# Attention's residual kept in its token tile, scaled and shifted on GpSimd, without the identity products behind Wo

## The chip, the cores and the metric

The kernel runs on one core of a Trainium2 chip (trn2). The metric is the device time of one execution in microseconds, as the median of several runs; shorter is better. Beside it stands the profile of one execution on that core, with every instruction of the five engines in time: TensorE (PE, with its weight loads as PEld), VectorE (DVE), ScalarE (ACT), GpSimd (POOL), and SyncE (SP), which issues most of the DMA.

## What is computed

Sixteen samples, each 256 tokens of 256 values in fp32, go through four layers one after the other. Only the second one changes here:

```
L0:  x = layernorm(x + up(expert(gelu(down(x))))) * gamma + beta     # an expert per sample
L1:  emb = silu(sin_emb(timestep)) @ W_ada + b_ada                   # (16, 512)
     scale, shift = split(emb)                                       # per sample, per value
     x = layernorm(x) * (1 + scale) + shift
     scores = (x Wq + bq)(x Wk + bk)^T / 4 + attention_bias ; masked ; softmax   # 16 heads
     x = x + (softmax(scores) (x Wv + bv)) @ Wo + bo                 # the residual in question
     x = x + gelu2(layernorm2(x) @ W1 + b1) @ W2 + b2
L2:  x = layernorm(x + one of three MLPs, chosen per sample) * gamma + beta
L3:  x = relu(x + dt * (derivatives of A*x and B*x on the 256x256 grid))
```

The attention bias is a side input of 16 x 16 x 256 x 256 fp32 values, 64 MB, read once.

## The kernel before

Weights stay on chip; a sample is two chunks of 128 tokens, so a tile [128, 2, 256] holds it ("token tile": tokens on partitions), and its transpose holds values on partitions. The work is written as generators, one per stage, which run over the 16 samples: `prepare` (L0 and the normalization of L1), `project` (q, k, v), `weigh` (scores, bias, softmax, over 64 groups of four heads), `attend` (transposing the weights and multiplying by v), `divide` (the softmax's division, the product with Wo and the residual; one call for each half of the heads), `enter` and `feed` (the MLP of L1), `end` (L2) and `step` (L3).

The order of instructions on all engines is fixed while the program is built. A planner, the class `Flow` (L91 to L167), keeps an estimated clock for each engine and for 7 of the PSUM banks; a generator yields the time from which it can go on, or a condition on `done`, and `flow.add(stage, at, per)` (L1103 to L1110) gives each stage an offset and a rate that decide which goes first. The estimates that stages report (`flow.pe(2.6)` and such) only make the order. On the chip each engine runs its list in that order and waits for semaphores. DMA issues are part of the same lists: SP issues the loads of x, expert weights, bias tiles (`load_side`), masks and branch weights and the stores of the output, ACT the first weights, and POOL the transfers that add the mask to a bias tile in place (`add_mask`, L508).

Lines that the change touches:
- `condition` (L486) computes scale and shift for all samples with values on partitions (`ps_a`, L491), `conditioned` (L500) adds the bias into `ada`.
- `prepare` normalizes x into `c_ln` (L567, 2 copies; it waits until `project` has transposed the tile of two samples before).
- `project` transposes it (`c_t`) and ACT applies scale and shift on the way out of PSUM (`c_xt`, L583, 3 copies). From `c_xt` come q, k and v. A gate (L577) holds it until the residual of three samples before is finished.
- `divide` uses `c_xt` a second time. The residual is needed with tokens on partitions, so it is transposed back by adding to the product with Wo:

```
for k in range(NC):                                                   # L814
    nc.tensor.matmul(ps_o[:, c, :], c_t[:, k, tok_], wo[:, k, :], start=k == 0, stop=False)
for k in range(NC):                                                   # L816
    nc.tensor.matmul(ps_o[:, c, k * P : (k + 1) * P], x_t[:, k, tok_], ident, start=False, ...)
```

- DVE then adds `bo` (L828) into `y`, a token tile of 4 copies, and takes its statistics; POOL computes the root and bias of the norm (L411 to L415). A gate (L810) holds `divide` until `step` of four samples before is done.

At the start, idle products (`idle`, L215) keep TensorE running while the first data come.

Of the kernel before, what the change touches and what calls it, by code (L numbers as in the profile page):

```python
# [19 lines left out]
P = 128  # L20
# [150 lines left out]
def chain_kernel(ctx: ExitStack, tc: tile.TileContext, t: dict, out: bass.AP):  # L171
# [31 lines left out]
        return at  # L203

    SIDES = 3
    xp = ctx.enter_context(tc.tile_pool(name="xp", bufs=2))
    side = ctx.enter_context(tc.tile_pool(name="side", bufs=SIDES))

# [42 lines left out]

    w_ada = wp.tile([P, NC, 2 * D], F32, name="w_ada", tag="d_w", bufs=1)
    nc.scalar.dma_start(out=w_ada, in_=chunked(t["W_ada"]))
    smalls = hp.tile([P, NC * S], F32, name="smalls", tag="d_ln", bufs=1)
    used = [0]

# [224 lines left out]
        nc.vector.tensor_copy(e_add, ps_b)  # L481
        return free("ps_b", flow.dve(0.2, flow.pe(0.5)))

    ps_a = {}

    def condition():  # L486

        ps_a[0] = misc("ps_a", [P, 4, B])
        for m in range(4):
            for k in range(NC):  # L490
                nc.tensor.matmul(  # L491
                    ps_a[0][:, m, :],
                    w_ada[:, k, m * P : (m + 1) * P],
                    silu[:, k, :],
                    start=k == 0,
                    stop=k == NC - 1,
                )
        flow.pe(2.0)

    def conditioned():  # L500
        nc.vector.tensor_tensor(ada, ps_a.pop(0), b_ada.unsqueeze(2).to_broadcast([P, 4, B]), ALU.add)
# [14 lines left out]
    def prepare():  # L516
        for b in range(B):
            w = e_ws.pop(b)
            xx = xs.pop(b)
            x, xt = xx[:, :, :D], xx[:, :, D:]  # L520
            ps_h = misc(f"a_h{b}", [A, S])
            for k in range(NC):
                nc.tensor.matmul(ps_h, w_down[:, k, :], xt[:, k, :], start=k == 0, stop=k == NC - 1)
            h1 = xp.tile([A, S], F32, name=f"a_h1{b}", tag="a_h1", bufs=1)
            nc.scalar.activation(h1, ps_h, AF.Gelu, bias=columns("down_b")[:A])
# [24 lines left out]
            nc.vector.tensor_tensor(x, ps_u, x, ALU.add)  # L550
            at = free(f"a_u{b}", flow.dve(0.7, flow.pe(0.9)))
            stat, at = take_stats(f"0_{b}", x, at)
            if b == 0:
                condition()
                idle(512, 512)
            yield at, 0
            tmp = xp.tile([P, NC, D], F32, name=f"b_tmp{b}", tag="b_tmp", bufs=1)
            at = normalized_affine(x, x, stat, ln0_g, ln0_b, tmp, b == 0)
            yield at, 0
            stat, at = take_stats(f"1_{b}", x, at)  # L560
            if b == 0:
                conditioned()
                masked.update((m, 0.0) for m in range(4))
            yield at, 0
            if b > 1:
                yield lambda: ("turned", b - 2) in done
            ln = xp.tile([P, NC, D], F32, name=f"c_ln{b}", tag="c_ln", bufs=2)  # L567
            lns[b] = ln, normalized(ln, x, stat, b == 0)
            done.add(("normal", b))

    def project():
        for b in range(B):
            yield lambda: ("normal", b) in done
            ln, at = lns.pop(b)
            yield at
            if b > 2:
                yield lambda: ("finish", b - 3) in done  # L577
            ps_t = misc(f"c_t{b}", [P, NC, S])
            at = transposed(ps_t, ln)
            done.add(("turned", b))  # L580
            x_t = wp.tile([P, NC, S], F32, name=f"c_xt{b}", tag="c_xt", bufs=3)
            for k in range(NC):
                nc.scalar.activation(  # L583
                    x_t[:, k, :],
# [47 lines left out]
            ready[b] = x_t, qz, k_t, va, sums  # L632
            done.add(("prepare", b))
            yield 0.0
            if b > 1:
# [29 lines left out]
    PR = 6  # L665
    MASK_FROM, MASK_BY = 2, 1

    def weigh():

        at = 0.0  # L670
        for m, (b, half, par) in enumerate(QUADS):
            if m % 4 == 0:
                yield lambda: ("prepare", b) in done
            _, qz, k_t, _, sums = ready[b]
            ps = []
            for i in range(4):
                yield 0.0, 1
# [70 lines left out]
    def attend():  # L748
        for m, (b, half, par) in enumerate(QUADS):
            if m % 4 == 0:  # L750
                yield lambda: ("values", b) in done
            for i in range(4):
                n = 4 * m + i
                yield lambda: ("weigh", n) in done
                pr, at = weights.pop(n)
                yield at
                ps_p = misc(f"c_pt{n}", [P, NC, S])
                at = transposed(ps_p, pr)
                p_t = hp.tile([P, NC, S], F32, name=f"c_pts{n}", tag="c_pts", bufs=4)
# [9 lines left out]
            ps_c, va = ctxs[b, half], ready[b][3]  # L769
            for k in range(NC):  # L770
                for i in range(4):
                    nc.tensor.matmul(  # L772
                        ps_c[32 * i : 32 * i + 32, :],
                        va[:, k, 4 * half + i, 2 * par : 2 * par + 2, :].rearrange("p e d -> p (e d)"),
                        turned[i][:, k, :],
                        start=par == 0 and k == 0,
                        stop=par == 1 and k == NC - 1,
                    )
            at = flow.pe(1.06)
            done.add(("gather", m))  # L780
            if par == 1:
                flow.add(divide(b, half), -9.0, 1e9)
            yield 0.0, 0

    def divide(b, half):


        x_t, _, _, _, sums = ready[b]
# [16 lines left out]
        done.add(("divide", 2 * b + half))  # L805
        yield flow.dve(0.34, at)
        if half == 0:
            return
        if b > 3:
            yield lambda: ("step", b - 4) in done  # L810
        ps_o = misc(f"c_o{b}", [P, NC, D])
        for c in range(NC):
            tok_ = slice(c * P, (c + 1) * P)
            for k in range(NC):  # L814
                nc.tensor.matmul(ps_o[:, c, :], c_t[:, k, tok_], wo[:, k, :], start=k == 0, stop=False)
            for k in range(NC):  # L816
                nc.tensor.matmul(
                    ps_o[:, c, k * P : (k + 1) * P],
                    x_t[:, k, tok_],
                    ident,  # L820
                    start=False,
                    stop=k == NC - 1,
                )
        at = flow.pe(2.6)
        del ready[b], c_ts[b]
        y = xp.tile([P, NC, D], F32, name=f"y{b}", tag="y", bufs=4)
        for c in range(NC):
            nc.vector.tensor_tensor(y[:, c, :], ps_o[:, c, :], bo, ALU.add)  # L828
        at = free(f"c_o{b}", flow.dve(0.67, at))
        stat, at = take_stats(f"2_{b}", y, at)  # L830
        ys[b], stats2[b] = y, (stat, at)
        done.add(("finish", b))
# [267 lines left out]
                    )  # L1100
                yield 0.0

    flow.add(prepare(), -2.56, 2.25)  # L1103
    flow.add(project(), -0.82, 5.7)
    flow.add(weigh(), 0, 21.2)
    flow.add(attend(), 0.96, 11.3)
    flow.add(enter(), -0.26, 0.44)
    flow.add(feed(), 2.45, 13.9)
    flow.add(end(), 2.77, 3.95)
    flow.add(step(), 4.22, 7.0)  # L1110
    flow.run()

def _arrays(inputs):
# [17 lines left out]
    for n in ("b_ada", "bq", "bk", "b1", "g2", "beta2"):  # L1131
# [21 lines left out]
        ),  # L1153
        "rows_a": np.concatenate([l0["ln_gamma"], l0["ln_beta"], l1["bv"], l1["bo"]]),
        "rows_b": np.concatenate([l1["b2"], l2["gamma"], l2["beta"], v["condB_dt"]]),
        **{k: l1[k] for k in ("W_ada", "Wo", "W1", "W2")},
        "W_qkv": np.concatenate([l1["Wq"], l1["Wk"], l1["Wv"]], 1),
        "W_branch": np.stack(
# [33 lines left out]
```

## Time and profile before

| | us |
|---|---|
| median of 3 runs (lowest, highest) | 923.14 (921.53, 926.4) |
| the profiled execution | 919.35 |
| its span, first to last instruction | 917.5 |
| mean granted TensorE clock in it | 0.990 of full speed |

The same lines group as follows in the profile (busy time is a union over time; the mean is that of one record, and an fp32 product leaves two records):

| group | records | busy us | mean ns |
|---|---|---|---|
| L815 PE, product with Wo | 128 | 33.8 | 387 |
| L817 PE, identity products | 128 | 19.5 | 275 |
| L828 DVE, y = c_o + bo, 128x256 | 32 | 12.1 | 419 |
| L583 ACT, c_xt from c_t, 128x256 | 32 | 16.0 | 550 |
| L446, L447 POOL on x, 128x512 | 15, 15 | 24.0, 19.1 | 1603, 1274 |
| L508 POOL, mask transfers issued | 60 | 80.8 | 1355 |

A line of busy times names the engine, its busy time and share, and the number of instructions. In a line of waits come the engine and line that stood still, what ended the wait, and the total, the number and the longest of these waits in us. A line of the list in order of time has the start, the time taken, engine, line, operation and tiles, and in brackets the idle time before it with what ended it. A line by stretch has the stretch, its length, the busy time of each engine with its number of instructions in parentheses, and at its end the granted clock, the share of DMA and GB/s.

### The profile page before, as it was taken

How to read it: one execution, taken by the hardware profiler on the slowest of the kernel's cores; microseconds unless marked ns; L12 is line 12 of the kernel's file. 1: busy time of each engine (PE TensorE's matmuls, PEld its weight loads, DVE VectorE, ACT ScalarE, POOL GpSimd, SP SyncE). 2: the span in 40 equal slices, each digit the busy share in tenths (PEclk: the TensorE clock that was granted, in tenths of full speed). 3: DMA queues.
4: the chain of work that ended last, by engine and by line, in shares of the span. 5: the costliest groups of instructions: out<-in, count | busy, mean ns of one | idle time of the engine just before them, and what ended most of it. 6: DMA issues, size and time to landing. Idle time of an engine off the chain costs nothing. (4 is left out here: it accounts for less than half of the span.)

```text
span 917.5 us, 18282 instructions
## 1 busy us (share of the span) xinstructions
PE 885.9 (97%) x6180; PEld 698.2 (76%) x6180; DVE 639.5 (70%) x2110; ACT 568.6 (62%) x1561; POOL 357.1 (39%) x500
## 2 busy tenths in 40 slices
PE   8899998999999999999999999999999999999997
PEld 3567675887777887778788777877887788778885
DVE  6677767767785767677686777768777785766343
ACT  2576667667665766758576675847667576656330
POOL 2233329142632616245261614526161543422331
PEclk8999999999999999999999999999999999999999
DMA  9389887776596767949676794967678486861010
GB/s 292 102 241 326 231 217 193 203 206 184 139 239 171 185 184 183 228 127 242 170 176 179 189 247 114 238 171 170 178 204 208 124 206 173 213 149 42 1 41 24
DMA packets 126555, 163.05 MB, mean 178 GB/s; under 512 B 12455, under 2 KB 86266, under 8 KB 126458
## 3 DMA queue, kind: packets, MB, share of 16 engines
q0 software_dynamic: 31680, 62.92, 34.1%
q1 hardware_dynamic: 93568, 96.92, 32.5%
q10 hardware_dynamic: 1209, 1.99, 0.7%
q8 instruction: 52, 0.85, 0.4%
q14 instruction: 46, 0.37, 0.1%
HBM read 94.69 MB, written 4.19 MB: 108 GB/s over the span
## 5 line engine op out<-in xcount | busy, mean ns | idle before, releaser
L718 ACT ACTIVATE c_pr<-c_sc,c_mx 128x256 f32<-128x256 f32 x512 | 255.1, 500 | 179.6 <-DVE c_mx L707 178.7
L707 DVE CUSTOM_DVE_ANT_0 c_sc<-c_s,side 128x256 f32<-128x256 f32 x512 | 194.4, 417 | 28.3 <-ACT e_o L1096 7.7
L454 PE MATMUL c_pt<-ident,c_pr 128*128 128x128 f32 x1024 | 143.5, 278 | 7.0 <-ACT c_pr L718 5.2
L454 PEld LDWEIGHTS c_pt<-ident,c_pr 128*128 128x128 f32 x1024 | 116.6, 142 | 34.6 <-ACT c_pr L718 12.7
L462 DVE COPY c_pts<-c_pt 128x512 f32<-128x512 f32 x183 | 122.8, 685 | 27.7 <-PE c_pt L454 27.4
L508 POOL DMA_DIRECT2D side<-neg x60 | 80.8, 1355 | 143.9 <-DMA side<-in_side 70.4
L411 POOL TENSOR_SCALAR rs<-mv 128x2 f32<-128x2 f32 x64 | 14.2, 221 | 293.6 <-DVE mv L408 291.7
L873 PE MATMUL d_f<-d_ht,w 128*128 128x256 f32 x512 | 121.4, 381 | 0.1
L903 PE MATMUL d_o<-w,d_z 128*128 128x256 f32 x512 | 116.0, 380 | 0.0
L903 PEld LDWEIGHTS d_o<-w,d_z 128*128 128x128 f32 x512 | 95.0, 190 | 12.3 <-issue 0.4
L873 PEld LDWEIGHTS d_f<-d_ht,w 128*128 128x128 f32 x512 | 92.8, 190 | 11.9 <-issue 0.9
L718 ACT ACTIVATION_READ_ACCUMULATOR c_pr<-c_sc,c_mx 128x1 f32 x512 | 96.1, 188 | 0.0
L689 PE MATMUL c_s<-c_kt,c_qz 32*128 32x256 f32 x1024 | 76.6, 401 | 0.8 <-DVE c_mx L707 0.4
L772 PE MATMUL c_c<-c_pts,c_va 128*32 128x256 f32 x1024 | 72.0, 387 | 3.3 <-DVE c_pts L462 2.9
L689 PEld LDWEIGHTS c_s<-c_kt,c_qz 32*128 32x128 f32 x1024 | 47.9, 184 | 23.5 <-issue 15.8
L892 ACT ACTIVATE d_f<-d_z 128x512 f32<-128x512 f32 x64 | 38.2, 597 | 28.5 <-DVE d_z L889 27.7
L772 PEld LDWEIGHTS c_c<-c_pts,c_va 128*32 128x32 f32 x1024 | 27.5, 109 | 33.4 <-issue 16.1
L911 DVE SCALAR_TENSOR_TENSOR y<-d_o,y 128x256 f32<-128x256 f32 x32 | 13.6, 424 | 55.5 <-PE d_o L903 55.5
L889 DVE TENSOR_SCALAR d_z<-d_f,cols 128x256 f32<-128x256 f32 x102 | 44.5, 477 | 10.7 <-PE d_f L873 9.9
L412 POOL TENSOR_TENSOR rs<-rs,inv_sqrt 128x2 f32<-128x2 f32 x64 | 46.0, 719 | 5.3
L464 ACT COPY c_pts<-c_pt 128x512 f32<-128x512 f32 x73 | 41.7, 572 | 8.8 <-PE c_pt L454 7.7
L896 DVE SCALAR_TENSOR_TENSOR d_z<-d_f,d_z 128x512 f32<-128x512 f32 x64 | 43.1, 673 | 3.5 <-ACT d_f L892 3.5
(152 smaller groups left out, 1602.2 us busy)
## 6 DMA issues: line engine op xcount, KB each, us to landing
side<-in_side SPq DMA_DIRECT2D x256, 256.0 KB, 5.6
side<-neg POOLq DMA_DIRECT2D x60, 1024.0 KB, 8.4
x<-in_x SPq DMA_DIRECT2D x16, 512.0 KB, 5.6
d_w<-in_W_branch SPq DMA_DIRECT2D x16, 512.0 KB, 6.4
out<-e_o SPq DMA_DIRECT2D x15, 256.0 KB, 4.9
w<-in_W SPq DMA_DIRECT2D x2, 1024.0 KB, 7.5
d_bout<-in_bl_branch SPq DMA_DIRECT2D x16, 128.0 KB, 5.8
grids<-in_grids SPq DMA_DIRECT2D x1, 1792.0 KB
```

What stands on the lines that cost most here:

```text
L412: nc.gpsimd.tensor_tensor(rs, rs, inv_sqrt, ALU.pow)
L454: nc.tensor.transpose(ps[:, k, c * P : (c + 1) * P], src[:, c, k * P : (k + 1) * P], ident)
L462: nc.vector.tensor_copy(dst, ps)
L508: nc.gpsimd.dma_start(out=sides[m].rearrange("p (h c) k -> p h (c k)", h=HB), in_=negs[m // 4].rearrange("p c k -> p (c k)").unsqueeze(1). ...
L689: nc.tensor.matmul(ps[i][:, c, :], qz[rows32, par, half, c * P : (c + 1) * P], k_t[rows32, half, :], start=b > 0, stop=b > 0 or c == NC - 1,)
L707: nc.vector.tensor_tensor_reduce(out=sc[:, c, :], in0=ps[i][:, c, :], in1=sb[:, i * NC + c, :], scale=-1.0, scalar=3.0e38, op0=ALU.add, op ...
L718: nc.scalar.activation(pr[:, c, :], sc[:, c, :], AF.Exp, bias=mx[:, c : c + 1], scale=-1.0, accum_out=sums[:, c, h : h + 1],)
L772: nc.tensor.matmul(ps_c[32 * i : 32 * i + 32, :], va[:, k, 4 * half + i, 2 * par : 2 * par + 2, :].rearrange("p e d -> p (e d)"), turned[i ...
L873: nc.tensor.matmul(ps_f[:, i, :], w1[:, k, f * P : (f + 1) * P], h_t[:, k, :], start=k == 0, stop=k == NC - 1,)
L889: nc.vector.tensor_scalar(z[:, i, :], ps_f[:, i, :], b1[:, f : f + 1], None, ALU.add)
L896: nc.vector.scalar_tensor_tensor(z, ps_f, 1.0, z, ALU.add, ALU.mult)
L903: nc.tensor.matmul(ps_o, us[f // 2][:, f % 2, c * P : (c + 1) * P], w2[:, f, :], start=f == 0, stop=f == NF - 1,)
```

## The change

The normalized token tile itself becomes the residual. It is no longer a tile of its own (`c_ln`) but the later `y`, with 7 copies. POOL multiplies it by (1 + scale) and adds shift + bo, both as rows that are the same on all partitions, when the first half of the heads is divided. For that, scale and shift are computed a second time, with samples on partitions: two products of 512 columns (`ps_r`) in `condition`; `modulated` adds 1, `b_ada` and `bo` on DVE, stores the 16 rows of 512 values to a DRAM scratch tensor and loads row 0 back, broadcast to 128 partitions; both DMAs are issued by ACT. The rows of later samples are loaded by SP in `divide`, one sample ahead, into one buffer. The product with Wo is alone in its accumulation, and DVE adds `ps_o` and `y` in one operation of 512 columns. Three gates between stages fall, one is added for the 7 copies, `c_xt` goes from 3 to 2 copies, and the offsets of six stages are set anew; so the planner's order changes throughout.

```diff
+    PR = 6
+    TOKENS = 7
+    dp = ctx.enter_context(tc.tile_pool(name="dp", bufs=1, space=bass.MemoryType.DRAM))
+    row_store = dp.tile([B, 2 * D], F32, name="row_store", tag="row_store")
...
     nc.scalar.dma_start(out=w_ada, in_=chunked(t["W_ada"]))
+    mod_rows = hp.tile([P, 2 * D], F32, name="mod_rows", tag="c_pr", bufs=PR)[:B]
+    nc.scalar.dma_start(out=mod_rows, in_=t["b_ada_row"].partition_broadcast(B))
...
-        flow.pe(2.0)
+        ps_r[0] = misc("ps_r", [P, 2 * D])
+        for k in range(NC):
+            nc.tensor.matmul(ps_r[0][:B], silu[:, k, :], w_ada[:, k, :], start=k == 0, stop=k == NC - 1)
+        flow.pe(3.8)
+
+    def modulated():
+
+        row, got = mod_rows, ps_r.pop(0)[:B]
+        nc.vector.scalar_tensor_tensor(row[:, :D], got[:, :D], 1.0, row[:, :D], ALU.add, ALU.add)
+        nc.vector.tensor_tensor(row[:, D:], got[:, D:], row[:, D:], ALU.add)
+        free("ps_r", flow.dve(0.8))
+        nc.vector.tensor_tensor(row[:, D:], row[:, D:], bo[:B], ALU.add)
+        flow.dve(0.4)
+        nc.scalar.dma_start(out=row_store, in_=row)
+        load_row(0, nc.scalar)
+
+    def load_row(b, engine):
+        mods[b] = wp.tile([P, 2 * D], F32, name=f"row{b}", tag="row", bufs=1)
+        engine.dma_start(out=mods[b], in_=row_store[b : b + 1, :].rearrange("b n -> (b n)").partition_broadcast(P))
...
-            if b > 1:
-                yield lambda: ("turned", b - 2) in done
-            ln = xp.tile([P, NC, D], F32, name=f"c_ln{b}", tag="c_ln", bufs=2)
+            if b >= TOKENS:
+                yield lambda: ("step", b - TOKENS) in done
+
+            ln = xp.tile([P, NC, D], F32, name=f"y{b}", tag="y", bufs=TOKENS)
             lns[b] = ln, normalized(ln, x, stat, b == 0)
+            if b == 0:
+                modulated()
...
-            if b > 2:
-                yield lambda: ("finish", b - 3) in done
...
-            x_t = wp.tile([P, NC, S], F32, name=f"c_xt{b}", tag="c_xt", bufs=3)
+            tokens[b] = ln
+            x_t = wp.tile([P, NC, S], F32, name=f"c_xt{b}", tag="c_xt", bufs=2)
...
         if half == 0:
+
+            y, row = tokens[b], mods.pop(b)
+            both = [P, NC, D]
+            nc.gpsimd.tensor_tensor(y, y, row[:, :D].unsqueeze(1).to_broadcast(both), ALU.mult)
+            nc.gpsimd.tensor_tensor(y, y, row[:, D:].unsqueeze(1).to_broadcast(both), ALU.add)
+            flow.pool(2.7)
             return
-        if b > 3:
-            yield lambda: ("step", b - 4) in done
+        if b + 1 < B:
+            load_row(b + 1, nc.sync)
...
             for k in range(NC):
-                nc.tensor.matmul(ps_o[:, c, :], c_t[:, k, tok_], wo[:, k, :], start=k == 0, stop=False)
-            for k in range(NC):
                 nc.tensor.matmul(
-                    ps_o[:, c, k * P : (k + 1) * P],
-                    x_t[:, k, tok_],
-                    ident,
-                    start=False,
-                    stop=k == NC - 1,
-                )
-        at = flow.pe(2.6)
+                    ps_o[:, c, :], c_t[:, k, tok_], wo[:, k, :], start=k == 0, stop=k == NC - 1
+                )
+        at = flow.pe(1.75)
...
-        y = xp.tile([P, NC, D], F32, name=f"y{b}", tag="y", bufs=4)
-        for c in range(NC):
-            nc.vector.tensor_tensor(y[:, c, :], ps_o[:, c, :], bo, ALU.add)
-        at = free(f"c_o{b}", flow.dve(0.67, at))
+        y = tokens.pop(b)
+        nc.vector.tensor_tensor(y, ps_o, y, ALU.add)
+        at = free(f"c_o{b}", flow.dve(0.68, at))
...
-    flow.add(prepare(), -2.56, 2.25)
-    flow.add(project(), -0.82, 5.7)
+    flow.add(prepare(), -2.54, 2.25)
+    flow.add(project(), -0.62, 5.7)
...
-    flow.add(attend(), 0.96, 11.3)
-    flow.add(enter(), -0.26, 0.44)
-    flow.add(feed(), 2.45, 13.9)
-    flow.add(end(), 2.77, 3.95)
-    flow.add(step(), 4.22, 7.0)
+    flow.add(attend(), 0.71, 11.3)
+    flow.add(enter(), -0.23, 0.44)
+    flow.add(feed(), 3.38, 13.9)
+    flow.add(end(), 2.6, 3.95)
+    flow.add(step(), 5.13, 7.0)
```

More of the change, by code (lines that the diff above doesn't have):

```diff
@@ L482, in expert_bias @@
         return free("ps_b", flow.dve(0.2, flow.pe(0.5)))
-    ps_a = {}
+    ps_a, ps_r, tokens, mods = {}, {}, {}, {}
     def condition():
@@ L575, in project @@
             yield at
-            if b > 2:
-                yield lambda: ("finish", b - 3) in done
             ps_t = misc(f"c_t{b}", [P, NC, S])
             at = transposed(ps_t, ln)
-            done.add(("turned", b))
-            x_t = wp.tile([P, NC, S], F32, name=f"c_xt{b}", tag="c_xt", bufs=3)
+            tokens[b] = ln
+            x_t = wp.tile([P, NC, S], F32, name=f"c_xt{b}", tag="c_xt", bufs=2)
             for k in range(NC):
@@ L631, in project @@
             sums = wp.tile([P, NC, H], F32, name=f"c_sum{b}", tag="c_sum")
-            ready[b] = x_t, qz, k_t, va, sums
+            ready[b] = qz, k_t, va, sums
             done.add(("prepare", b))
@@ L664, in chain_kernel @@
     weights, turned, c_ts, ctxs = {}, {}, {}, {}
-    PR = 6
     MASK_FROM, MASK_BY = 2, 1
@@ L673, in weigh @@
                 yield lambda: ("prepare", b) in done
-            _, qz, k_t, _, sums = ready[b]
+            qz, k_t, _, sums = ready[b]
             ps = []
@@ L768, in attend @@
                 ctxs[b, half] = pp.tile([P, S], F32, name=f"c_c{b}_{half}", tag="c_c", bufs=1)
-            ps_c, va = ctxs[b, half], ready[b][3]
+            ps_c, va = ctxs[b, half], ready[b][2]
             for k in range(NC):
@@ L785, in divide @@
     def divide(b, half):
-        x_t, _, _, _, sums = ready[b]
+        _, _, _, sums = ready[b]
         ps_c = ctxs.pop((b, half))
@@ L1155, in _arrays @@
         "rows_b": np.concatenate([l1["b2"], l2["gamma"], l2["beta"], v["condB_dt"]]),
+        "b_ada_row": l1["b_ada"],
         **{k: l1[k] for k in ("W_ada", "Wo", "W1", "W2")},
```

## The prediction

> **What bounds the kernel now.** I read the busy table first, then busy time by stage, then who waited for whom, and last the list of instructions in order of time around the lines that change. Engine, busy time with its share of the span, instructions:
>
> ```profile
> PE 885.9 (97%) x6180; PEld 698.2 (76%) x6180; DVE 639.5 (70%) x2110; ACT 568.6 (62%) x1561; POOL 357.1 (39%) x500
> ```
>
> TensorE (PE) is busy for 885.9 of 917.5 us, which leaves 31.6 us without a matmul. By stage (stretch, its length, then busy time of PE, PEld, DVE, ACT and POOL):
>
> ```profile
> 0.00:24.00 24.00, 19.94 (x56) 9.36 (x56) 15.98 (x65) 7.18 (x11) 5.99 (x19) 0.86 0.91 289
> 24.00:40.00 16.00, 13.70 (x80) 9.96 (x84) 9.37 (x31) 7.86 (x23) 2.94 (x6) 0.89 0.06 18
> 100.00:200.00 100.00, 94.43 (x679) 71.73 (x678) 71.47 (x249) 68.12 (x193) 42.76 (x57) 0.98 0.76 197
> 500.00:600.00 100.00, 99.32 (x731) 80.07 (x729) 73.98 (x248) 68.25 (x185) 45.31 (x62) 1.00 0.75 188
> ```
>
> From 300 us on TensorE rests for under 1 us in 100. The holes are in the start, in the filling of the pipeline up to about 300, and at the end. Busy matmul time could hide a stall, because matmuls are pipelined, so I ask what PE waited for:
>
> ```profile
> PE c_pt L454 <- ACT c_pr L718: 5.2, 11, 1.8
> PE e_t L454 <- POOL y L447: 2.9, 2, 2.2
> PE c_c L772 <- DVE c_pts L462: 2.9, 4, 1.1
> ```
>
> All waits named for PE add up to some 26 us, and the largest is 5.2. ACT, DVE and POOL wait for each other far longer (ACT 178.7 us for the row minima of L707), but with slack. So the body is bound by the amount of matmul work in order, and a microsecond taken from it there should shorten the span. The start is different: a chain across ACT, DVE and PE sets it.
>
> **What the Trainium skill says.** "Perfetto Trace Analysis", section Identifying the Most-Contended Engine, warns that matmul occupancy is no measure of roofline and prefers the share of weight loads. Here that is 76%, and the list of waits, not the 97%, is what my reading rests on. "TensorE: Matmul & The Clock Gate", section Architectural detail, says that ACT and DVE are strict first-in first-out; the trace agrees, since ACT's first table load comes only after the held-back issue of w_qkv (7.04 to 7.44). "DMA: Bandwidth & Descriptors", section Anatomy of one DMA, puts about 2 us of fixed cost on a DMA, most of it the receipt of the write, and says that the issuing sequencer does the waiting; the fastest write in this trace (128 KB of out) lands in 1.7 us. "GPSIMD Engine Reference", section Key points, says that GpSimd shares its SBUF interfaces with DVE; L446 on 128x512 took 1270 ns at least and 1762 in the median, L447 1273, which fits.
>
> **The change, part by part.**
>
> Removed from PE: 8 identity products per sample. Their busy time, 19.5 us, counts overlap. The true pitch is read from PE in order of time:
>
> ```profile
> 857.10 1.03 PE L815 MATMUL c_o<-wo,c_cts 128*128 128x256 f32 x4
> 857.96 0.61 PE L817 MATMUL c_o<-ident,c_xt 128*128 128x128 f32 x4
> 858.41 1.03 PE L815 MATMUL c_o<-wo,c_cts 128*128 128x256 f32 x4
> 859.27 0.61 PE L817 MATMUL c_o<-ident,c_xt 128*128 128x128 f32 x4
> 859.72 3.62 PE L903 MATMUL d_o<-w,d_z 128*128 128x256 f32 x16
> ```
>
> From 857.96 to 858.41 is 0.45, and from 859.27 to 859.72 again. Two per sample, 16 samples: 2 x 0.45 x 16 = 14.4 us off PE.
>
> Added to PE at the start: ps_r, two products of 512 columns. The idle products of that width on L222 took 0.94 a pass at a slow clock (3.76 us for 4 passes), and 8 passes of 256 columns at full clock take 1.89, or 0.47 for 512. So 1.9 to 3.8 us. I take the upper, and hide it behind DVE's norm chain, which ends at 21.27 while ps_r would end near 20.3. If DVE were quicker, it would show on c_t, which PE could still start between 22 and 27.5 (see next).
>
> Added to ACT at the start, in front of everything else. Of the lines for ACT:
>
> ```profile
> 13.38 1.28 ACT L525 ACT_TABLE_LOAD   x1
> 21.77 0.47 ACT L525 ACTIVATE a_h<-a_h,cols 64x256 f32<-64x256 f32 x1 [7.10 <-PE a_h L523]
> 23.44 1.02 ACT L583 ACTIVATE c_xt<-c_t,ada 128x256 f32<-128x256 f32 x2 [1.21 <-PE c_t L454]
> ```
>
> In the new order the store of the 16 rows and the load of row 0 stand on ACT's queue between the tanh of the time embedding and this table load. The store waits for DVE's last row operation. The load waits until the store has landed in DRAM. Behind them wait the Gelu table, a_h of sample 1 and c_xt of sample 0, and behind c_xt all projections. Step by step:
> - The b_ada load takes an earlier slot in ACT's DMA order, and the builder makes rows_a and w_qkv wait for older transfers (x of sample 0 and w_ada). w_ada, issued at 2.74, lands 5.5 later, about 8.3; the first Gelu table then starts near 9.1 instead of 7.53 and the Gelu about 0.5 later than 9.72: +0.5 (0 to 1).
> - Three DVE operations on 16x256 behind c_ln, priced by the 128x256 row of L828 (419 ns): 1.3. Rows are ready at 21.27 + 0.5 + 1.3 = 23.1.
> - Store: 2.5 from issue to landing (1.7 is the fastest write seen, 4.9 the median of out): 25.6. Issue of the load 0.4: 26.0.
> - Table load 1.28, Gelu 0.47: c_xt at 27.7, against 23.44. That is **+4.3 us**, from 3 to 7.
>
> Moved at the start: the score products of sample 0 now stand before c_v, which before came first (PE 27.64 to 29.5). Scores wait only for c_kt, which ACT finishes at 28.88 while they began at 30.33. And c_v (1.89) now lies where PE stood idle 2.3 us between 24 and 40. I take -1.5 (0 to -2.3).
>
> DVE: 32 additions of 0.419 become 16 of about 0.69 (as y at L1028): -2.4 us. The written order also turns 31 copies c_pts from ACT to DVE (+21.2) and 22 d_z from DVE to ACT (-10.5); with the smaller ones DVE gains about 11 us, ACT loses about 7. DVE then has 650 of some 906, 72%: not on the path, because PE waited for it about 7 us after the start.
>
> POOL: 2 operations of 128x512 per sample, each 1.27 to 1.79, so 2.5 to 3.6 a pair, 41 to 57 us in all; POOL goes from 39% to about 45%. Nothing: they stand half a sample (some 27 us of PE work between the two divisions) ahead of the addition that reads them. Behind a pair on POOL's queue stand most often the root and the bias of the third norm, then a mask transfer, and for those the cover is PE work too: by PE's order, at the durations above, d_y to e_t has 40 to 56 us in the body (50.9 before).
>
> DMA: 16 row loads of 256 KB (4.2 of 163 MB), 15 on SP. Each takes an issue slot (0.4) ahead of a side load, and waits for POOL's pair of the sample before. SP stood 392.9 us waiting for DVE at L307, so the slot is free; the row has half a sample to land, rows_a took 5.0. If the row came late, POOL would stop and every norm with it.
>
> Buffers and waits: the token tile has 7 copies, three gates fall, c_xt goes to 2. I read the cover between producers and consumers off both PE orders: d_t to d_f rises from 7.6 to about 19 us, c_t to c_q from 2.4 to about 4.9, c_r to c_o from 1.0 to 3.5; d_g to d_y falls from 4.1 to about 3, a_h to a_e is shorter early, and two places (c_r to c_o of samples 0 and 14) have only 0.6. I take 0 for new and lost stalls, from -4 to +8. The end is the same sequence from d_f of sample 15 on: 0.
>
> Sum: -14.4 + 4.3 - 1.5 + 0 = **-11.6 us**. Span 917.5 becomes 905.9; the execution 919.35, with 1.85 around its span, becomes 907.8. The median of the three runs, 923.14, is 3.8 above the profiled one; I carry the difference over: **911.5 us**.
>
> **The rivals.**
> 1. Start and body both dearer: store and load 4.9 each way in effect (+7), stalls +3 to +5. -14.4 + 7 - 0.5 + 3 = -5, up to -1: 918 to 922. For it: landing under load in this trace is mostly 4 to 6. Against: the queues are near empty from 24 us on (DMA share 0.06).
> 2. Slower: POOL's pair stands in front of a norm that PE needs. At the root of a norm (L411) POOL so far arrives early, and waits 291.7 us for DVE. If of each pair's 2.9 us some 1.5 comes through to PE per sample, 24 us are lost and the sum is +12: 935. It decides from 11.6 / 16 = 0.73 us per sample on (no gain), and is slower by 0.5% from 1.0. Against: e_t waited for POOL only about 5.6 us in all, and the cover above.
> 3. The gain does not arrive: ACT and DVE set the pace, PE merely idles more. It gives 923 + 2.8 = 926. Against: PE waited for them for a few us.
> 4. More gain: the fuller cover takes away part of the 10 us of stalls between 60 and 300: down to 904 or less.
>
> **How the numbers follow.** Main case 0.58 (906 to 917), rival 1 0.16, rival 2 0.12, rival 3 0.05, rival 4 0.09. About 0.5% (4.6 us) is what a measurement can tell from no change. Faster, below 918.5: main, rival 4, and a fifth of rival 1: 0.70. Same: the rest of rival 1 and half of rival 3: 0.16. Slower: 0.14. Range: 904 leaves out half of rival 4, 926 leaves out rival 2 and half of 3: 904 to 926.
>
> **What would show it.** Right: PE has no 128x128 identity rows on c_o, and its busy sum is about 16 to 18 us less; c_xt starts near 27.7 with ACT waiting for the store; PE stays above 99% from 300 to 700; the addition of y is not held by POOL. Wrong: PE waits for POOL's norms or for y above 10 us in all; POOL waits for the row load; PE between 100 and 700 falls below 98%; or c_xt starts after 31.

## The result, and the profile after

The changed kernel takes 929.65 us in the median of six runs (926.77 to 932.13), the kernel before 923.29 beside it. The ratio is 1.0065, with a 95% interval of 1.0044 to 1.0086: slower by about 6.4 us, where 11.6 us less were forecast. The profiled execution took 926.77 us with a span of 925.0 (before 919.35 and 917.5).

The busy table of the kernel after (engine, busy time with its share of the span, instructions):

```profile
PE 886.4 (96%) x6056; PEld 680.6 (74%) x6056; DVE 657.7 (71%) x2106; ACT 563.6 (61%) x1552; POOL 399.1 (43%) x532
```

TensorE (PE) has 124 instructions fewer, and its busy time has not fallen at all (885.9 before). The removed products did go: measured from one PE start to the next, they cost 14.5 us in the trace of before, and there is nothing in their place after. In order of time at the end of the run, the product of Wo now goes straight on into d_o:

```profile
866.36 1.89 PE L845 MATMUL c_o<-wo,c_cts 128*128 128x256 f32 x8
868.08 4.26 PE L926 MATMUL d_o<-w,d_z 128*128 128x256 f32 x19
```

So more time passes at other groups of products. The same sums from start to start, which hold the wait before the next product too, name them: c_q +6.8, c_t +4.4, c_s +3.7, ps_r +3.5 (new), d_o +2.7, c_k +2.4, c_pt and c_o +1.9 each. By stage (the same stretches and columns as before the change: busy time of PE, PEld, DVE, ACT, POOL; granted PE clock; DMA share; GB/s):

```profile
0.00:24.00 24.00, 19.48 (x53) 9.13 (x54) 16.15 (x65) 4.87 (x7) 6.00 (x19) 0.86 0.89 281
24.00:40.00 16.00, 12.65 (x58) 9.06 (x59) 3.08 (x12) 6.91 (x13) 0.00 (x0) 0.79 0.15 49
...
100.00:200.00 100.00, 96.37 (x670) 73.17 (x671) 79.49 (x261) 68.67 (x197) 47.18 (x62) 0.98 0.82 214
...
500.00:600.00 100.00, 98.71 (x706) 76.25 (x705) 72.21 (x233) 65.57 (x185) 49.98 (x64) 1.00 0.76 195
```

Two things are to be seen. From 24 to 40 us PE starts 58 matmuls where it started 80, and its clock is lower (0.79; 0.89 before). And from 500 to 600 it rests for 1.29 us instead of 0.68. What PE waited for, of the whole run:

```profile
PE c_pt L460 <- ACT c_pr L742: 3.7, 10, 1.5
PE a_e L564 <- ACT a_h L549: 3.6, 2, 3.3
PE c_k L622 <- DVE c_mx L731: 3.0, 1, 3.0
```

The second is new, 3.3 us in one piece at the start, and so is the third, 3.0 us in one piece at 98 us, to which section 4 of the experiments comes back.

**The start.** ScalarE (ACT) in order of time:

```profile
22.55 0.33 ACTq L517 DMA_DIRECT2D row_store<-mod_rows  x1
26.57 0.35 ACTq L522 DMA_DIRECT2D row<-row_store  x1
26.95 1.28 ACT L549 ACT_TABLE_LOAD   x1 [13.46 <-DMA row_store<-mod_rows]
28.25 0.47 ACT L549 ACTIVATE a_h<-a_h,cols 64x256 f32<-64x256 f32 x1
28.62 1.01 ACT L608 ACTIVATE c_xt<-c_t,ada 128x256 f32<-128x256 f32 x2
```

The chain is the one of the prediction, link by link. The rows were ready earlier than forecast (22.55 for 23.1), the store took 4.0 us until the load could be issued (2.5 forecast), and c_xt began at 28.62 (27.7 forecast, 23.44 before). TensorE behind it:

```profile
28.77 1.11 PE L564 MATMUL a_e<-a_h,e_w 64*64 64x256 f32 x2 [3.35 <-ACT a_h L549]
29.82 3.78 PE L622 MATMUL c_q<-c_xt,w_qkv 128*128 128x256 f32 x8
33.39 2.63 PE L622 MATMUL c_k<-c_xt,w_qkv 128*128 128x256 f32 x8
```

Before, the eight products c_q took 2.02 and c_k 1.89. After the rest of 3.35 us they step at 427 ns, and from the fifth of c_k on at 216: the clock was halved for some 12 products, which is 2.5 us more. "TensorE: Matmul & The Clock Gate" of the Trainium skill (Part 1: The HAM clock gate) says that an idle window of about 3.4 us brings the half clock; this rest agrees with the size, others in these traces do not (last section). The first score products c_s start at 36.83, 6.5 us later than before (30.33), though c_v no longer stands ahead of them.

**The body.** Between 300 and 700 us, what the weight loads (PEld) of c_pt, the transposes of the softmax, sat idle for. In the kernel before:

```profile
L454 PEld LDWEIGHTS c_pt<-ident,c_pr x472: 138/141/144, 300.0 to 696.1; 128*128 128x128 f32 x158
its engine sat idle before it (us, times) until:
  issue: 2.9, 7
```

In the kernel after:

```profile
L460 PEld LDWEIGHTS c_pt<-ident,c_pr x478: 137/140/143, 300.5 to 699.9; 128*128 128x128 f32 x160
its engine sat idle before it (us, times) until:
  issue: 9.7, 26
  DVE c_mx L731: 4.6, 10
  ACT c_pr L742: 3.5, 9
  ACT d_z L910: 2.1, 6
  ACT c_spr L817: 1.9, 5
  ACT c_pts L470: 1.0, 3
```

Most of this is no loss. When c_c, c_s or a_h comes ahead of c_pt, the weight load rests 0.41, 0.33 or 0.38 us, whatever the profile names, and with the same lengths in half_both below: the 2.9 us before are seven times 0.41 behind c_c, and after nearly all but the line of c_mx has these three lengths. The new order puts c_pt behind such products more often, and other products less; c_c and c_s themselves take 16.0 and 17.2 us in four steady samples in both orders, from start to start. The waits for c_mx are another matter. With two more, in order of time:

```profile
397.42 0.86 PEld L460 LDWEIGHTS c_pt<-ident,c_pr 128*128 128x128 f32 x8 [0.45 <-DVE c_mx L731]
398.73 0.42 PEld L460 LDWEIGHTS d_t<-ident,d_ln 128*128 128x128 f32 x4 [0.46 <-DVE d_z L919]
399.50 1.59 PEld L665 LDWEIGHTS c_v<-w_qkv,c_xt 128*128 128x128 f32 x8 [0.34 <-ACT c_kt L653]
422.41 0.42 PEld L460 LDWEIGHTS c_pt<-ident,c_pr 128*128 128x128 f32 x4 [0.47 <-DVE c_mx L731]
```

These four waits come once in each of five samples and set their product back by 0.21, 0.39, 0.27 and 0.40 us, 1.27 us a sample. None waits for its input: the softmax that c_pt reads had been ready for 8.3 and 4.0 us, d_ln for 0.65, and c_v reads c_xt, which c_q and c_k had read before. What they wait for is the accumulator, the PSUM bank that they write into. By the planner's allotment of its seven PSUM banks, these c_pt get the bank of a score product c_s, d_t that of a d_f, c_v that of c_k, and c_mx, d_z and c_kt, which the profile names, are what reads those banks out. Between 300 and 700 us no product of the kernel before waits in this way.

None of this stands high in a list of waits. Its effect is read from the period, the time between the starts of c_q of neighbouring samples. Of four samples, c_q (min, median and max of one product in ns, then the first and the last start) before:

```profile
L597 PE MATMUL c_q<-c_xt,w_qkv x32: 379/379/380, 431.6 to 593.0; 128*128 128x256 f32 x32
```

and after:

```profile
L622 PE MATMUL c_q<-c_xt,w_qkv x32: 379/379/483, 447.8 to 611.2; 128*128 128x256 f32 x32
```

From the first start to the last (three periods and the 1.5 us within a sample) it was 161.4 us and is 163.4. A sample takes 53.25 us before and 54.1 after (four periods from 339 to 556 us; the third here is already 53.6), though it has 0.9 us of products less: 1.75 us per steady sample are lost, and the four waits above are 1.27 of them.

### The profile page after: what moved, and what is told of

It reads as the page before. It is cut to its first block, busy times and chain, and to the rows that moved or that the text cites. A ratio compares the mean times of both kernels' runs of the same rounds, so it can differ in the third digit from the quotient of the medians.

```text
span 925.0 us, 18078 instructions
## 1 busy us (share of the span) xinstructions
PE 886.4 (96%) x6056; PEld 680.6 (74%) x6056; DVE 657.7 (71%) x2106; ACT 563.6 (61%) x1552; POOL 399.1 (43%) x532
## 5 line engine op out<-in xcount | busy, mean ns | idle before, releaser
L460 PE MATMUL c_pt<-ident,c_pr 128*128 128x128 f32 x1024 | 150.6, 280 | 5.6 <-ACT c_pr L742 3.7
L460 PEld LDWEIGHTS c_pt<-ident,c_pr 128*128 128x128 f32 x1024 | 112.9, 141 | 55.0 <-issue 21.5
L468 DVE COPY c_pts<-c_pt 128x512 f32<-128x512 f32 x214 | 143.8, 685 | 12.2 <-PE c_pt L460 11.0
L713 PE MATMUL c_s<-c_kt,c_qz 32*128 32x256 f32 x1024 | 78.6, 408 | 4.2 <-DVE c_mx L731 1.8
L713 PEld LDWEIGHTS c_s<-c_kt,c_qz 32*128 32x128 f32 x1024 | 49.6, 187 | 27.2 <-issue 11.3
L731 DVE DVE_READ_ACCUMULATOR2_ANT c_mx<- 128x1 f32 x512 | 42.8, 84 | 0.0
L1001 POOL TENSOR_TENSOR y<-y,d_bout 128x256 f32<-128x256 f32 x32 | 26.7, 981 | 30.8 <-PE d_t L460 20.9
```

The lines of the kernel that those rows point to most:

```text
L460: nc.tensor.transpose(ps[:, k, c * P : (c + 1) * P], src[:, c, k * P : (k + 1) * P], ident)
L468: nc.vector.tensor_copy(dst, ps)
L713: nc.tensor.matmul(ps[i][:, c, :], qz[rows32, par, half, c * P : (c + 1) * P], k_t[rows32, half, :], start=b > 0, stop=b > 0 or c == NC - 1,)
L731: nc.vector.tensor_tensor_reduce(out=sc[:, c, :], in0=ps[i][:, c, :], in1=sb[:, i * NC + c, :], scale=-1.0, scalar=3.0e38, op0=ALU.add, op ...
```

## The experiments

Three theories went in. A: the new written order of TensorE's work loses the gain. B: GpSimd's pair of operations comes in front of norms that PE needs. C: the start, held by the store and the load on ScalarE's queue. All ratios are to the kernel before.

**1. Which of the three.** `new_old_order` is the whole change with the planner's estimates, gates and start offsets of before, and PE's order is then that of before, less the identity products:

```
+ flow.pe(2.6) at Wo, flow.pe(2.0) at ps_r; no flow.pool for the pair, none for the rows
+ gates ("turned", b-2), ("finish", b-3), ("step", b-4) as before
+ flow.add offsets -2.56, -0.82, 0, 0.96, -0.26, 2.45, 2.77, 4.22
```

> The changed residual (token tile, GpSimd pair, rows from DRAM, no identity products) with the planner's estimates, gates and offsets of the kernel before, so that TensorE's order is that of the kernel before without the identity products. Theory A (the new order of instructions loses the gain, some 1.7 us per sample): the gain comes back, less the longer start: 923.3 - 14.4 + 6.5 = about 915 us, 912 to 919. Theory B (the GpSimd pair itself costs, by holding up norms and masks or VectorE's port): no better than the changed kernel, 926 to 931. Theory C (the start alone is what is wrong): about 917 as well, so A and C are told apart by the period of a sample: under A 52.4 us here against 54.1 in the changed kernel, under C the same in both.

Measured: 917.79 us, ratio 0.9940 (0.9923 to 0.9957). It is faster than before, and 11.9 us faster than the change as made, by what the planner writes alone: the order, and with it the engine of some copies. `ident_new_order` turns it round, the order of after with the work of before:

```
- nc.gpsimd.tensor_tensor(y, y, row...) x2
+ identity products with c_xt (3 copies) behind Wo; bo added by VectorE in two operations
+ row loads of half the size, not read
```

> The changed kernel's order, with the identity products put back behind Wo, bo added by VectorE in two operations, and the GpSimd pair left out (the row loads stay, at half the size, and nobody reads them). Theory A: the order is what is slow, and TensorE in it has slack of its own: identity products cost 14.4 us at most, and less where TensorE waits for the softmax: 936 to 944 us. Theory B: products back (+14.4) and the pair's cost gone (some 15): about 929.

Measured: 937.65, 1.0145 (1.0112 to 1.0179), with a period of 54.9 us against 53.25. The start with the store and load is in this time too; the period is not touched by it. A holds in both directions. `no_pair` is the change without GpSimd's two operations (the scale and shift of the residual are left out):

```
- nc.gpsimd.tensor_tensor(y, y, row[:, :D]..., ALU.mult)
- nc.gpsimd.tensor_tensor(y, y, row[:, D:]..., ALU.add)
```

> The changed kernel without GpSimd's two operations per sample; it leaves out scale and shift of the residual, all else and the order are the same. Theory A: no difference, 928 to 931 us. Theory B: the pair is the cause, 912 to 918.

Measured: 930.06, 1.0078 (1.0051 to 1.0106). The pair costs nothing; B falls. `rows_pool` moves the first store and load off ScalarE's queue:

```
- nc.scalar.dma_start(out=row_store, in_=row); load_row(0, nc.scalar)
+ nc.gpsimd.dma_start(out=row_store, in_=row); load_row(0, nc.gpsimd)
```

> The changed kernel with the store of the 16 rows and the load of row 0 issued by GpSimd instead of ScalarE, so that ScalarE goes on to the table load and the Gelu at once. Theory C (ScalarE's wait for the round trip through DRAM, and TensorE running at half clock after it, are a loss that stays to the end): 6 to 8 us less than the changed kernel, 922 to 924, with c_xt of sample 0 starting before 25 us instead of 28.6. If the delay at the start is taken up by later waits: 928 to 931.

Measured: 924.39, 1.0011 (1.0000 to 1.0022), 5.3 us less than the change. PE then does c_q and c_k in 2.02 and 1.89 us, as in the kernel before, and c_s begins at 29.11, 1.2 us before the kernel before:

```profile
24.56 2.02 PE L622 MATMUL c_q<-c_xt,w_qkv 128*128 128x256 f32 x8
26.41 1.89 PE L622 MATMUL c_k<-c_xt,w_qkv 128*128 128x256 f32 x8
28.14 1.04 PE L708 MATMUL c_s<-neg,ident_b 128*128 128x256 bf16 x8
29.11 1.15 PE L713 MATMUL c_s<-c_kt,c_qz 32*128 32x256 f32 x16
```

**2. Both repairs together, and the price of the removal.** `old_rows_pool` joins the edits of `new_old_order` and `rows_pool`.

> The kernel after with the planner's estimates, gates and offsets of before (TensorE does its work in the order of before), and with the store of the rows and the load of row 0 issued on GpSimd's queue instead of ScalarE's. If the two losses found so far are separate, they add: 929.65 - 11.9 (order) - 5.3 (start) = 912.5 us, a ratio of 0.988 to before, and the first c_q near 24.6 us. If the later start was hidden in the old order (the filling has slack there), it stays at 917 to 918. If it falls below 911, the start was costing more in the old order than in the new.

Measured: 912.63, 0.9884 (0.9852 to 0.9915). The two losses add, as expected, and this version beats both kernels, by 11.9 and some 17 us. `no_ident` is the kernel before with nothing but the identity products taken out (the residual of attention is left out):

```
- nc.tensor.matmul(ps_o[:, c, k * P : (k + 1) * P], x_t[:, k, tok_], ident, ...)
```

> The kernel before with the eight identity products of each sample taken out and nothing else changed: order, start and placing as before. It leaves out the residual of attention. The prediction's first term says -14.4 us, so 908.7 to 909.5 and a ratio near 0.984, with a period of about 52.4 us per sample (53.25 before). If TensorE's idle products hid a wait (the third rival: the gain does not arrive in whole even where nothing else changes), it gives -5 to -10, 913 to 918.

Measured: 910.56, 0.9858 (0.9822 to 0.9894): 14.0 us less than before. The working of the removal (14.4) was right. In `old_rows_pool` the body is as in the kernel before, with a sample 0.9 us shorter:

```profile
L623 PE MATMUL c_q<-c_xt,w_qkv x32: 379/379/379, 432.7 to 591.2; 128*128 128x256 f32 x32
```

158.5 us for what took 161.4, that is 52.4 a sample.

**3. What in the order.** The order comes from estimates and offsets, and it comes with a placing of copies on VectorE or ScalarE. `old_placing` keeps PE's order of after and puts the copies where the kernel before has them:

```
+ ON_DVE = {"c_pts": {...}, "d_xt": {...}, "d_z": {...}}   # as in the kernel before
- if flow.clock["DVE"] + 0.6 <= flow.clock["ACT"] + 0.56:
+ if n in ON_DVE[kind]:
```

> The kernel after, with TensorE's order of after kept instruction for instruction, but with the copies out of PSUM (c_pts, d_xt) and the bias additions d_z on the engine, VectorE or ScalarE, on which the kernel before has them (29 plus 60 copies c_pts, 12 d_xt and 29 pairs d_z change engine). If the loss of some 12 us comes from the load moved to VectorE, it gives 918 to 921. If it comes from TensorE's order itself, it stays at 927 to 932, or rises where a placing that was made for another order now misses.

Measured: 953.86, 1.0325 (1.0296 to 1.0354). `old_offsets` has the new estimates with the old offsets (the eight `flow.add` numbers above).

> The kernel after with the eight start offsets of before for the chains (feed 2.45 for 3.38, step 4.22 for 5.13, attend 0.96 for 0.71 and small ones), and the new estimates kept. The offsets fix how far the chains stand apart in the whole run, the estimates only a part of a microsecond per sample. If the offsets are what cost the gain, it gives 916 to 921. If the estimates are (1.75 for 2.6 at Wo, 2.7 for the new pair on GpSimd, 3.8 at the start), it stays at 926 to 932.

Measured: 965.96, 1.0462 (1.0430 to 1.0494). The first expectation allowed for a rise, but gave no size; the second missed, on the far side. Neither part of the old setting repairs the new order; mixed, they are worse than either whole. What PE's orders have in common: the work between a head's score products and the transposes of its softmax is short in after and in `old_offsets` (median 9 to 13 us per sample in the steady part; 22 before). Three runs tried whether that is the cause, all by attend's offset:

```
attend_late       after:          flow.add(attend(), 0.71, 11.3) -> 2.0
attend_late2      after:          flow.add(attend(), 0.71, 11.3) -> 1.8
old_attend_early  old_rows_pool:  flow.add(attend(), 0.96, 11.3) -> 0.5
```

> The kernel after with one number changed: the start offset of the chain that transposes the softmax weights and multiplies them with V (attend) is 2.0 instead of 0.71. By TensorE's order at the matmul times of the trace, the work between the score products of a head (c_s) and the transposes of its softmax (c_pt) was 22 us in the median per sample in the kernel before (smallest 17), and is 9 in the kernel after (smallest 4 to 5); with this offset it is 17 to 21 from sample 6 on (smallest 13 to 16), and 7 to 15 in samples 0 to 5, as in after. Other chains shift a little. If the short cover between c_s and c_pt is what made the gain of the removal disappear, the steady period falls from 54.1 us per sample to 52.4 to 52.9, the waits for c_pr and c_mx in front of c_pt nearly vanish between 300 and 700, and the time falls by some 8 to 12 us, to 918 to 922. If the loss is spread over the other short covers, or is any order's own accident, it stays at 926 to 935.

> As the run before with the offset at 1.8: another order of TensorE, with nearly the same cover between c_s and c_pt (18 to 21 us in the median from sample 4 on, smallest 13 to 15). If the cover decides, the period and the time are those of the run before to within 0.5 us and 4 us: 917 to 922. If the other covers or accidents of the order decide, the two runs differ by more, or both stay above 926.

> The reverse: the kernel with the planner's numbers of before and the rows on GpSimd's queue (912.63 us, cover between c_s and c_pt 22 us), with attend's offset at 0.5 instead of 0.96. The cover falls to 8.6 us in the median (smallest 3.9), as in the kernel after. If the short cover costs what after lost, the period rises from 52.4 to about 54 and the time by 10 to 18 us, to 922 to 930, with waits for c_pr and c_mx in front of c_pt. If the cover does not matter, it stays at 911 to 915.

Measured: 936.63 (1.0152, 1.0122 to 1.0182), 931.62 (1.0099, 1.0076 to 1.0122) and 926.01 (1.0025, 1.0009 to 1.0041). With the wide cover the later periods are mostly 53.2 to 53.6 us instead of 54.1, not 52.4, and earlier one or two samples lose more than is won (between 270 and 400 us they take 58.7 to 64.5). With the cover made short in the good order the period rises by 1.0, from 52.4 to 53.4. So the short cover costs something, but less than was lost, and as the sole cause it falls. `before_attend` asks whether only the changed kernel is so sensitive: the kernel before with a single number moved.

```
- flow.add(attend(), 0.96, 11.3)
+ flow.add(attend(), 0.90, 11.3)
```

> The kernel before with one number of the planner changed: attend's start offset 0.90 instead of 0.96. No work is added or removed. The order of TensorE changes in places (median cover between c_s and c_pt 18 to 22 us instead of 22, d_g to d_y 2.0 to 2.7 instead of 4.1). If the order of before is a narrow good one and nearly any other costs, it gives 928 to 940 with a period above 53.8 us. If orders of about the same covers are worth the same, it stays at 921 to 926.

Measured: 946.44, 1.0246 (1.0206 to 1.0286). The same work, 22 us slower, more than expected. Its periods run from 50.0 to 58.5 us, and PE meets waits such as this in order of time, which the kernel before does not have:

```profile
317.37 0.41 PE L797 MATMUL c_r<-ident,c_spr 128*128 128x128 f32 x2
319.29 1.10 PE L1079 MATMUL e_d<-e_b,grids 128*128 128x256 f32 x4 [1.51 <-DVE c_mx L707]
```

This too is a bank: e_d does not read c_mx, and here it gets the bank of a c_s.

**4. Late results, or TensorE's own sequence.** Orders and placings are kept on every engine here; the softmax is made cheaper, so that its results come sooner. In each of these half the columns of the softmax are left out.

```
half_rowmin   c_sc: out, in0 and in1 [..., : S // 2]; the exponentials read the half twice
half_exp      c_pr[:, c, : S // 2] from c_sc[:, c, : S // 2]; the transposes read the half twice
half_both     both of them; _old: the same in old_rows_pool
```

> The kernel after, its order and placing kept on every engine, with VectorE's row minima of the scores (c_sc, 256 columns, two per head) taken over 128 columns; ScalarE's exponentials still write 256 columns and read the 128 twice. It leaves out half the columns of the scores in the softmax. It takes some 32 x 0.1 to 0.15, or 3 to 5 us per sample, off VectorE, which is 71% busy, and nothing off TensorE. If TensorE loses its time to results that come late from VectorE, the period falls from 54.1 us towards 52.4 and the time by 8 to 18 us, to 912 to 922. If the loss lies inside TensorE (issue, weight loads, the order's own length) or with ScalarE, it stays at 926 to 930.

> The control: the same halved row minima (half the columns of the scores are left out) in the kernel with the planner's numbers of before and the rows on GpSimd's queue (912.63 us). Its period is 52.4 us with few waits, so the relief should be worth little there: 0 to 4 us in the filling of the pipeline, 908 to 913. If it gains as much as the run before (over 8 us), the relief is worth the same in any order, and says nothing on the order of after.

> The kernel after, order and placing kept on every engine, with ScalarE's exponentials (c_pr, two of 256 columns per head, 503 ns each) over 128 columns; TensorE's transposes of the softmax read these 128 columns twice, so it does the same work. It leaves out half the columns of the softmax. It takes some 32 x 0.12, about 4 us per sample, off ScalarE. If TensorE's steady loss is waiting for ScalarE (17.2 us of weight-load waits between 300 and 700, the largest part named), the period falls from 54.1 to 53.0 or less and the time to 910 to 918. If it is TensorE's own order, the period stays at 53.8 to 54.1 and the time at 920 to 929, what falls being in the filling.

> The kernel after with both halved: VectorE's row minima and ScalarE's exponentials (half the columns of the softmax are left out). If late results of the two engines together are the loss, the period falls to 52.4 to 52.8 and the time to 900 to 912. If the period stays above 53.5, the loss lies in TensorE's own sequence and the time is 916 to 924.

> The control: both halved (half the columns of the softmax are left out) in the kernel with the planner's numbers of before and the rows on GpSimd's queue (912.63 us). The period should stay at 52.2 to 52.4, and the time fall only by what the filling gives, to 904 to 912. What is left between this and half_both, beyond 5.3 us for the start, is loss that no relief of the softmax takes away.

| | time, us | ratio (95%) | steady period, us |
|---|---|---|---|
| after | 929.65 | 1.0065 (1.0044 to 1.0086) | 54.1 |
| half_rowmin | 922.07 | 0.9993 (0.9969 to 1.0016) | 53.9 |
| half_exp | 924.31 | 1.0007 (0.9994 to 1.0021) | 53.8 |
| half_both | 917.69 | 0.9938 (0.9919 to 0.9956) | 53.6 |
| old_rows_pool | 912.63 | 0.9884 (0.9852 to 0.9915) | 52.4 |
| half_rowmin_old | 912.92 | 0.9888 (0.9847 to 0.9928) | 52.3 |
| half_both_old | 906.35 | 0.9824 (0.9796 to 0.9853) | 52.3 |

The relief takes 12.0 us off the new order and 6.3 off the old one. Between half_both and half_both_old 11.3 us are left, and with the start's 5.3 taken off, 6.0, where the orders differed by 11.8 without relief (924.39 to 912.63). So about half of what the order costs goes with the time that VectorE and ScalarE spend on the softmax. The steady period gives back 0.5 of its 1.75 us: the waits for c_mx fall from 0.61 to 0.26 us a sample and that for c_kt from 0.27 to 0.05, while d_t still waits for d_z, which was not made cheaper (0.46 for 0.39). Of the 17.2 us that half_exp's expectation counts as waits for ScalarE, 8.5 stand on c_pt and are the rests of fixed length. The largest single wait of what stays is in the filling of the pipeline, in half_both:

```profile
97.12 0.29 DVE L731 CUSTOM_DVE_ANT_0 c_sc<-c_s,side 128x128 f32<-128x128 f32 x1 [6.52 <-DMA side<-neg]
97.78 3.75 PE L622 MATMUL c_k<-c_xt,w_qkv 128*128 128x256 f32 x8 [4.07 <-DVE c_mx L731]
```

c_k does not read c_mx; it gets the bank of a score product whose row minimum waits for its bias tile, to which the mask is still being added. The wait is 4.07 us, and c_k's eight products then take 3.75 us for 1.89, at half the clock: some 5.9 us that a cheaper softmax cannot take away. It is the wait of 3.0 us in the list of the kernel after, and 4.52 us in `rows_pool`; half_both_old has none like it, with 0.9 us as its longest wait there.

## Why the prediction was wrong

The differences add up, each from its own pair of runs: removal -14.0, rows and pair themselves +2.1 (912.63 against 910.56), store and load on ScalarE's queue +5.3, order +11.9. The sum is +5.3; +6.4 was measured, and the intervals of the single runs reach up to 3.3 us to either side. In `old_rows_pool` c_q starts at 26.14 us, 2.1 later than in `no_ident`: that is where the +2.1 of the rows would lie.

- **Covers and waits, "0 for new and lost stalls, from -4 to +8".** This step failed, and alone turned the sign: it was +11.9. Covers were compared between producers and consumers of data, and each was held to be safe above zero; when an accumulator comes free was not asked. In the trace of after that is what fails: 1.27 of the 1.75 us lost per steady sample, and 3.0 us in one piece in the filling, are waits for a PSUM bank that has not been read out. The cover from c_s to c_pt was not compared either and fell from 22 us to 9, but in the steady part the c_pt that waited had their inputs ready for 4 us and more, and widening it did not repair the order. The runs show that the order of before is a narrow good one: 0.06 on one offset cost 22 us, and no other order that was tried came near it.
- **"From 300 us on TensorE rests for under 1 us in 100", hence bound by matmul work.** As a reading of before it was right: in the old order 0.9 us of work less gave a period 0.9 us shorter (52.4 for 53.25). It doesn't carry over to another order. The sign named against the forecast, PE busy below 98%, never came either: 98.5 to 98.9 between 300 and 600, while 1.75 us of each sample were lost. Busy time hides such waits, and the period shows them.
- **ACT's start, "+4.3 us, from 3 to 7".** The mechanism was right, and the term too small, though inside its range. c_xt came 5.2 later, c_q 5.8 and c_s 6.5; against the same kernel with the rows on GpSimd's queue it is 5.3 in time. The store's 4.0 us for 2.5 is the larger part. The half clock behind PE's rest was not in the sum at all. (The table load at 7.53 us that was named for ACT's strict order is put down to the landing of `up`; the table load that stood 13.46 us behind the store shows that order better.)
- **"-1.5" for the score products ahead of c_v.** With the rows off ScalarE's queue it is there (c_s 1.2 us early). With them on it, the half clock took it.
- **Identity products -14.4.** Right: 14.0 by the run, 14.5 by the starts. **ps_r hidden:** it took 3.5 us of PE's time (1.9 to 3.8 forecast), and with the rows on GpSimd's queue c_q starts 0.5 us later than before.
- **POOL's pair and the row loads at nothing.** The pair is shown to be free (930.06 without it), and GpSimd never waited for a row. Rival 2 had its place and its mechanism wrong. Rival 1 was near on the start (+7), and far too low on stalls (+3 to +5). Rival 3, with its 926 nearest to the time, had a cause (ACT and DVE set the pace) that holds for about half of the order's loss.

What stays open: that the banks are the cause is read from the traces and from the planner's allotment, at the places named. No run gave the new order another allotment of banks, so what the order would cost without these waits was not measured. About 0.5 us of the steady 1.75, and how the rest of the filling shares in the 11.9 us, are not itemized, and the far larger losses of `old_placing` and `old_offsets` were not followed.

## What to carry to other kernels

When a change makes a planner write a new order, the order is a change of its own: run the new work in the old order first, and the old work in the new one, before the two are judged together. A few tenths of a microsecond at a few places of every sample appear neither in the busy share nor among the large waits; measure the period between two starts of the same product in neighbouring samples instead. Of each wait, ask whether the instruction named makes an input or reads out the accumulator that is wanted next: a cover between producer and consumer says nothing of the second. A store to DRAM and a load that depends on it belong on a queue behind which nothing urgent stands: here GpSimd's for ScalarE's was worth 5.3 us.

## What was not expected of the hardware

A 32 KB store through DRAM held the issue of its load by 4.0 us (22.55 to 26.57), above the roughly 2 us of fixed cost that "DMA: Bandwidth & Descriptors" (Anatomy of one DMA) gives for one transfer on GpSimd's path (this store was issued by ScalarE); DMA traffic was still draining then. And a single rest of TensorE of 3.35 us halved its clock for about 12 products of 256 columns (427 ns each for 216), so that the rest cost 2.5 us beyond its own length. The length of a rest alone does not tell: in the same trace one of 1.80 us, to 92.76, was followed by a granted clock of 0.53 from 92.8 to 96.4, and one of 3.01 us, to 100.84, by c_k at 216 ns. So the 3.4 us of the page is not the limit here.
